# Four-layer image model, selective scan: partitions re-tiled from 128 channels to 4 state groups by 32 channels

## Chip, cores and metric

The kernel runs on one core of a Trainium2 chip. The metric is the device time of one execution in microseconds (us). The kernel before takes 22,114.64 us, the median of three runs (22,108.16 to 22,117.55).

## The reference

The input is `x` of 8 images, 56 x 56 pixels, 192 channels, in fp32. Four layers follow each other, each added to its input after a group normalisation: a gated Toeplitz layer, window attention, a depthwise 3x3 convolution, and a selective scan (384 inner channels `d`, 16 states `n`, 4 scan directions `k`). The change touches the last one:

```python
delta = jax.nn.softplus(delta + delta_bias[None, :, :, None])
dA = jnp.exp(delta[:, :, :, None, :] * A[None, :, :, :, None])
dBu = (delta * u)[:, :, :, None, :] * Bm[:, :, None, :, :]
def comb(e1, e2):
    a1, b1 = e1
    a2, b2 = e2
    return (a1 * a2, a2 * b1 + b2)
_, hs = jax.lax.associative_scan(comb, (dA, dBu), axis=-1)
y = jnp.einsum('bkdnl,bknl->bkdl', hs, Cm)
return y + Dp[None, :, :, None] * u
```

So for each channel and each state there is one recurrence along 3,136 tokens; B and C depend on state and token, not on the channel; delta and u depend on channel and token, not on the state; at the end the 16 states are summed.

## The kernel before

**The first phase** does the Toeplitz layer's transforms for all images and, beside them, the `front` of image 0. **The scan phase** then goes through 224 chunks (8 images, 4 directions called slots, 7 chunks of `CH` = 448 tokens). A chunk has 3 blocks `d` of 128 channels and 8 pairs `k` of states: 5,376 pairs in all, 24 to a chunk. One (chunk, d), that is 8 pairs, is called a block here; there are 672.

**One pair** is one tile of 128 channels by 2 states x 448 tokens:

- `inject` (L1000, GpSimd): `ring` = du x B. `ring` has 6 buffers; it runs two pairs ahead (`ahead`).
- `decay` (L1017, ScalarE): two Exp of delta, with the state's A as scale, into `ps_a` in PSUM (2 buffers), one pair ahead.
- `scan` (L1026, VectorE): the recurrence, in place in `ps_a` or in `ring`.
- `times_c` (L1032): `hc` = states x C, on VectorE, and on GpSimd for k in (1, 4, 6), where it is issued one pair later. `hc` has 4 buffers.
- `add_up` (L1047, TensorE): two matmuls by the identity add both states into `ps_y`, 16 per block. It is issued two pairs later.
- `sums` (L1057, L1059, VectorE): adds `ps_y` to `ysum`, once a block. `keep_state` (L1039) and `initial` (L1007) are small ScalarE copies.

**Its inputs** come through SyncE's DMA queue, in the order of the program. B and C are loaded broadcast: `load_bc` (L973) copies two state rows to all 128 partitions, once for each pair. `load_delta` (L984) brings delta of a chunk, `load_xc` (L978) brings u, and `times_x` (L988, GpSimd, 1 per block) makes du = delta x u.

**Beside the scan** runs the `front` of the next image: `gate`, `attention`, `conv2`, `inner`, and `steps`, which makes B, C (`bc_d`) and delta (`dl_d`) in DRAM, 14 chunk steps per image; Softplus is at L883 and the stores of delta at L886. `finish` normalises and projects the image before. Both are Python generators. A planner (`Parts`) keeps a modelled clock for each engine, and after each pair it inserts as many of their pieces as fit in its limits; nothing is scheduled at run time, each engine executes its instructions in program order. The planner counts `add_up` as 1.1 us of TensorE per pair. Its check of whether a piece fits looks at VectorE, ScalarE and TensorE, not at GpSimd.

Of the kernel before, what the change touches and what calls it, by code (L numbers as in the profile page):

```python
# [15 lines left out]
F32 = mybir.dt.float32  # L16
AF = mybir.ActivationFunctionType
# [6 lines left out]
L = H * W  # L24
# [3 lines left out]
CH = 448  # L28
# [8 lines left out]
NP = NS // NG  # L37
SLAB, SLAB_F = 10048, 2688
# [44 lines left out]
def model(ctx: ExitStack, tc: tile.TileContext, a: dict, out: bass.AP):  # L83
# [5 lines left out]
    def load_const(pool, name, eng=None):  # L89
        t = pool.tile(list(a[name].shape), F32, name=name + "_sb")  # L90
        (eng or nc.sync).dma_start(out=t, in_=a[name])
        return t
# [18 lines left out]
        for n, shape in (("xc", [128, ND, L]), ("bc", [64, L]))  # L111
    )
    dl_d = [[dram.tile([128, ND, L], F32, name=f"dl{s}_{b}") for b in range(B)] for s in range(4)]
# [181 lines left out]
    with (  # L295
# [5 lines left out]
        ln_g, ln_b, w_out, w_dt = (load_const(wp, n) for n in ("ln_g", "ln_b", "w_out", "w_dt"))  # L301
        negA = load_const(wp, "A_logs")
# [542 lines left out]
        def steps(b):  # L845

            w_x, xc, rc, dl = carve(slab, 128, (2, ND, 128), (2, ND, CH), (2, CH), (2, ND, CH))
            nc.sync.dma_start(out=w_x, in_=a["w_x"])
            todo = [(o, j) for o in (1, 0) for j in range(NCH)]

            def load_x(n):
                o, j = todo[n]
                nc.sync.dma_start(out=xc[:, n % 2], in_=xc_d[o][b][:, :, j * CH : (j + 1) * CH])

            load_x(0)
            yield 0, 0, 8.0
            for n, (o, j) in enumerate(todo):
                tok = slice(j * CH, (j + 1) * CH)
                if n + 1 < len(todo):
                    load_x(n + 1)  # L860
                yield 0, 1
                p = bank()
                for d in range(ND):
                    nc.tensor.matmul(p[:, :CH], w_x[:, o, d, :], xc[:, n % 2, d, :], start=d == 0, stop=d == ND - 1)
                yield 1, 0
                nc.scalar.copy(rc[:, n % 2, :], p[:, :CH])
                nc.sync.dma_start(out=bc_d[o][b][:, tok], in_=rc[64:, n % 2, :])
                for d in range(ND):
                    yield 0, 2
                    held = []  # L870
                    for s in range(2):
                        row = slice(32 * s, 32 * s + R)
                        held.append(bank())
                        nc.tensor.matmul(
                            held[s][:, :CH], w_dt[row, o, d * 128 : (d + 1) * 128], rc[row, n % 2, :], start=True, stop=True
                        )
                    yield 2, 0
                    for s in range(2):
                        nc.scalar.activation(
                            dl[:, s, d, :], held[s][:, :CH], AF.Identity, bias=dt_b[:, 2 * o + s, d : d + 1]  # L880
                        )
                yield 0, 0
                nc.scalar.activation(dl, dl, AF.Softplus)  # L883
                usual_functions()
                for s in range(2):
                    nc.sync.dma_start(out=dl_d[2 * o + s][b][:, :, tok], in_=dl[:, s])  # L886
                made.add((b, o, j))
            yield 0, 0
# [76 lines left out]
        bms, cms, deltas, dus, xcs, states, hss, das, hcs, yps, xds = ({} for _ in range(11))  # L965

        def load_bc(i, k):
            b, slot, j = chunks[i]
            for ts, name, r0 in ((bms, "bm", 0), (cms, "cm", NS)):
                ts[i, k] = bcp.tile([128, NG, CH], F32, name=name)  # L970
                r = slot % 2 * 32 + r0 + NG * k
                src = bc_d[slot // 2][b][r : r + NG, j * CH : (j + 1) * CH]
                nc.sync.dma_start(out=ts[i, k], in_=src.unsqueeze(0).to_broadcast([128, NG, CH]))  # L973

        def load_xc(i, d):
            b, slot, j = chunks[i]
            t = sp.tile([128, CH], F32, name="xcd", bufs=3)
            nc.sync.dma_start(out=t, in_=xc_d[slot // 2][b][:, d, j * CH : (j + 1) * CH])  # L978
            return t

        def load_delta(i):
            b, slot, j = chunks[i]
            delta = deltas[i] = delta2[:, i % 2]
            nc.sync.dma_start(out=delta[:, :, 1 : CH + 1], in_=dl_d[slot][b][:, :, j * CH : (j + 1) * CH])  # L984

        def times_x(i, d):
            du = dus[i, d] = sp.tile([128, 1, CH], F32, name="du", bufs=3)
            nc.gpsimd.tensor_mul(du[:, 0, :], deltas[i][:, d, 1 : CH + 1], xcs.pop((i, d)))  # L988

        def tokens(i):  # L990

            return (slice(0, CH), CH, 0) if chunks[i][1] % 2 else (slice(1, CH + 1), 0, CH)

        def on_pool(d, k):
            return k in (1, 4, 6)

        def inject(g):
            i, d, k = pairs[g]
            hs = hss[g] = ring[:, g % 6]
            nc.gpsimd.tensor_mul(hs[:, :, tokens(i)[0]], dus[i, d].to_broadcast([128, NG, CH]), bms[i, k])  # L1000
# [8 lines left out]
        def decay(g):  # L1009
            i, d, k = pairs[g]  # L1010
            slot = chunks[i][1]
            dA = psa.tile([128, 1024], F32, name="ps_a")
            dA = das[g] = dA[:, : NG * (CH + 1)].rearrange("p (n t) -> p n t", n=NG)
            at = slot % 2
            for n in range(NG):
                c = NG * k + n
                nc.scalar.activation(  # L1017
                    dA[:, n, :], deltas[i][:, d, at : at + CH + 1], AF.Exp, scale=negA[:, slot, d, c : c + 1]
                )
# [8 lines left out]
        def times_c(g):  # L1028
            i, d, k = pairs[g]
            h = hss[g] if on_pool(d, k) else das[g]  # L1030
            hc = hcs[g] = sp.tile([128, NG, CH], F32, name="hc", bufs=4)
            (nc.gpsimd if on_pool(d, k) else nc.vector).tensor_mul(hc, h[:, :, tokens(i)[0]], cms[i, k])  # L1032
# [8 lines left out]
        def add_up(g):  # L1041

            i, d, k = pairs[g]
            if k == 0:
                yps[i, d] = psy.tile([128, 512], F32, name="ps_y")
            for n in range(NG):
                nc.tensor.matmul(  # L1047
                    yps[i, d][:, :CH], ident, hcs[g][:, n, :], start=k + n == 0, stop=k + n == NP + NG - 2
                )
# [105 lines left out]
        bcp = own.enter_context(tc.tile_pool(name="bc", bufs=NP))  # L1155
        ysum = wp2.tile([128, ND, L], F32, name="ysum")
        ring = wp2.tile([128, 6, NG, CH + 1], F32, name="ring")
        delta2 = wp2.tile([128, 2, ND, CH + 2], F32, name="delta2")

        for u in range(2):  # L1160
            nc.gpsimd.memset(delta2[:, u, :, 0 : CH + 2 : CH + 1], 1e30)
# [3 lines left out]
        with tc.manual_schedule():  # L1165
            for k in range(NP):
                load_bc(0, k)
            load_delta(0)
            for d in range(ND):
                xcs[0, d] = load_xc(0, d)  # L1170
                times_x(0, d)
# [10 lines left out]
            def take(g):  # L1182
                times_c(g)
                after = scanned[g], summed[g - 4] if g > 3 else 0.0
                taken[g] = run("P", 2.0, *after) if on_pool(*pairs[g][1:]) else run("D", 1.09, *after)
# [11 lines left out]
            for g, (i, d, k) in enumerate(pairs):  # L1197
# [5 lines left out]
                if more and d == 1 and k == 0:  # L1203
                    b1, slot1, j1 = chunks[i + 1]
                    while (b1, slot1 // 2, j1) not in made:
                        parts.step(anything, ahead_of)
                    load_delta(i + 1)
                    for e in range(2):
                        xcs[i + 1, e] = load_xc(i + 1, e)
                if more and (d, k) == (2, 0):  # L1210
                    xcs[i + 1, 2] = load_xc(i + 1, 2)
                if more and (d, k) in ((1, 6), (1, 7), (2, 6)):
                    times_x(i + 1, k - 6 if d == 1 else 2)
                    run("P", 1.08)
# [17 lines left out]
                if g and pd == ND - 1 and pi + 1 < len(chunks):  # L1232
                    load_bc(pi + 1, pk)
# [17 lines left out]
                if g >= 2:  # L1251
                    add_up(g - 2)
                    summed[g - 2] = run("E", 1.1, taken[g - 2])
            if on_pool(d, k):
                times_c(last)
            for g in (last - 1, last):
                add_up(g)
# [6 lines left out]
def constants():  # L1264
# [22 lines left out]
    return {"ident": np.eye(128, dtype=f), "gmat": gmat, "pos": pos, "masks": masks}  # L1287


def layouts(i):  # L1290
# [47 lines left out]
    a["A_logs"] = np.asarray(i[p + "A_logs"]).reshape(4, ND, 128, NS)[order].transpose(2, 0, 1, 3)  # L1338
# [24 lines left out]
```

## Time and profile before

| what | value |
|---|---|
| median of the runs | 22,114.64 us |
| span of the profiled execution | 22,054.7 us |
| scan phase, first to last scan | 3,429.8 to 22,017.6 us: 18,587.8 us |
| one image of the scan phase, images 0 to 6 | 2,347 to 2,393 us |
| the last image (no front beside it) | 2,030 us |
| VectorE busy in the scan phase | 15,930 us |
| TensorE clock granted, mean | 0.891 |

The page cuts the span into 40 slices and gives the busy tenths of each engine. PE is TensorE's matmuls, PEld its weight loads, DVE is VectorE, ACT ScalarE, POOL GpSimd. An fp32 matmul of the program stands in the trace as two instructions, each with a weight load.

```profile
## 2 busy tenths in 40 slices
PE   7878977788887889888988888788988898887667
...
DVE  2122117997799779987899789977998789977998
...
POOL 0000007987889778987888788878898789878999
PEclk9588868999999989999999999898999999998888
```

From slice 7 on the scan runs. DVE and POOL go up and down together with a period of about 4.3 slices, one image: high while the front is in `gate` and `attention`, low in `conv2`, `inner` and `steps`. In the last slices, without a front, POOL is at its highest and PE at its lowest. The chain of work that ended last covers under 1% of the span here, so it says nothing on the whole; the reading goes by stretches and by waits.

### The profile page before, as it was taken

Reading aid. Unit: us, or ns where it says so; the run is one execution under the profiler, and the core shown is the slowest. Engines: PE = TensorE matmul, PEld = TensorE weight load, DVE = VectorE, ACT = ScalarE, POOL = GpSimd, SP = SyncE. Lnnn points to the kernel's source line nnn. Section 1 sums busy time; section 2 is a strip of 40 time slices with the busy share of each in tenths; the row PEclk is TensorE's granted clock in tenths of the full one; section 3 lists DMA queues with packets and bytes.
Section 4 is the critical chain, followed back from the end, with each engine's and each line's share of the span. In section 5 each row is a group of like instructions: output and inputs, shape, how many; then the busy total and the mean of one; then the engine's idle time right before and its main releaser. Section 6 shows DMA issues by size and latency. Waiting matters only on the chain. (4 is left out here: it accounts for less than half of the span.)

```text
span 22054.7 us, 196675 instructions
## 1 busy us (share of the span) xinstructions
PE 18328.2 (83%) x58396; PEld 9752.3 (44%) x58396; DVE 16637.5 (75%) x13276; ACT 12126.1 (55%) x28153; POOL 16068.5 (73%) x8503
## 2 busy tenths in 40 slices
PE   7878977788887889888988888788988898887667
PEld 4845654334443444344443444344444444343333
DVE  2122117997799779987899789977998789977998
ACT  3125114655666465656665576656565666556554
POOL 0000007987889778987888788878898789878999
PEclk9588868999999989999999999898999999998888
DMA  3832575344644465345644464345534564445433
GB/s 88 239 99 49 177 186 165 122 130 162 185 138 125 145 194 152 121 129 180 185 124 128 159 196 137 123 147 189 159 117 131 176 186 125 126 151 184 129 127 110
DMA packets 2419588, 3249.95 MB, mean 147 GB/s; under 512 B 917598, under 2 KB 2361024, under 8 KB 2387554
## 3 DMA queue, kind: packets, MB, share of 16 engines
q1 hardware_dynamic: 2398292, 3121.12, 46.8%
q0 software_dynamic: 15520, 116.14, 1.4%
q8 instruction: 463, 7.59, 0.1%
q14 instruction: 609, 4.99, 0.1%
q10 hardware_dynamic: 4704, 0.12, 0.0%
HBM read 2661.35 MB, written 575.48 MB: 147 GB/s over the span
## 5 line engine op out<-in xcount | busy, mean ns | idle before, releaser
L1000 POOL TENSOR_TENSOR ring<-du,bm 128x896 f32<-128x896 f32 x5376 | 11104.3, 2092 | 17.3 <-DMA bm<-bc 10.1
L1047 PE MATMUL ps_y<-hc,ident_sb 128*128 128x448 f32 x21504 | 9809.0, 591 | 688.5 <-POOL hc L1032 620.9
L1026 DVE TENSOR_TENSOR_SCAN ps_a<-ps_a,ring 128x898 f32<-128x898 f32 x3360 | 6795.9, 2023 | 756.3 <-ACT ps_a L1017 295.2
L1017 ACT ACTIVATE ps_a<-delta,A_logs_sb 128x449 f32<-128x449 f32 x10752 | 6860.2, 638 | 327.8 <-DVE ring L1026 45.5
L1047 PEld LDWEIGHTS ps_y<-hc,ident_sb 128*128 128x128 f32 x21504 | 4281.7, 207 | 4745.4 <-issue 3574.5
L1032 POOL TENSOR_TENSOR hc<-ring,cm 128x896 f32<-128x896 f32 x2016 | 3947.5, 1958 | 2086.0 <-DVE ring L1026 991.9
L1032 DVE TENSOR_TENSOR hc<-ps_a,cm 128x896 f32<-128x896 f32 x3360 | 3668.4, 1092 | 1166.5 <-PE ps_y L1047 880.1
L1026 DVE TENSOR_TENSOR_SCAN ring<-ps_a,ring 128x898 f32<-128x898 f32 x2016 | 4063.3, 2016 | 276.6 <-ACT state L1039 121.0
L1039 ACT COPY state<-ps_a 128x2 f32<-128x2 f32 x3359 | 529.9, 158 | 4120.2 <-DVE hc L1032 4111.2
L278 DVE COPY tzx<-ps_tz 112x448 f32<-112x448 f32 x432 | 269.9, 625 | 1421.9 <-PE ps_tz L272 1289.2
L286 POOL DMA_DIRECT2D o<-tzx x192 | 97.4, 514 | 1686.4 <-DVE tzx L278 1552.5
L272 PE MATMUL ps_tz<-tzx,tm 112*112 112x112 f32 x4608 | 1031.7, 404 | 287.2 <-DMA tm<-ext 272.9
L272 PEld LDWEIGHTS ps_tz<-tzx,tm 112*112 112x112 f32 x4608 | 1028.1, 319 | 326.6 <-issue 320.5
L815 PE MATMUL ps_f<-slab 128*128 128x448 f32 x2646 | 1092.8, 549 | 55.3 <-DMA slab<-dg_d 48.1
L645 PE MATMUL ps_f<-ident_sb,slab 98*98 98x98 f32 x1344 | 335.8, 315 | 558.1 <-ACT slab L638 558.1
L747 PE MATMUL ps_f<-slab 96*96 96x448 f32 x1764 | 729.8, 549 | 42.5 <-DVE slab L734 42.5
L815 PEld LDWEIGHTS ps_f<-slab 128*128 128x128 f32 x2646 | 508.5, 193 | 555.8 <-issue 502.2
L77 PE MATMUL ps_f<-slab 96*96 96x448 f32 (+6 forms) x2306 | 737.8, 501 | 9.3 <-DMA slab<-x 4.1
L988 POOL TENSOR_TENSOR du<-delta,xcd 128x448 f32<-128x448 f32 x672 | 711.0, 1058 | 22.2 <-DMA slab<-in_x_dram 22.2
L1039 ACT COPY state<-ring 128x2 f32<-128x2 f32 x2016 | 378.7, 188 | 609.7 <-DVE ring L1026 581.0
L630 ACT ACTIVATE slab<-slab,mxs 98x98 f32<-98x98 f32 x1344 | 487.6, 364 | 357.8 <-DVE mxs L627 357.8
L482 PE MATMUL ps_f<-ident_sb,slab 112*96 112x112 f32 x4704 | 531.1, 267 | 138.3 <-DVE slab L490 95.0
(218 smaller groups left out, 16966.9 us busy)
## 6 DMA issues: line engine op xcount, KB each, us to landing
bm<-bc SPq DMA_DIRECT2D x1792, 448.0 KB
cm<-bc SPq DMA_DIRECT2D x1792, 448.0 KB
xcd<-xc SPq DMA_DIRECT2D x840, 224.0 KB
dl<-slab SPq DMA_DIRECT2D x224, 672.0 KB
delta<-dl SPq DMA_DIRECT2D x224, 672.0 KB
tzx<-qv SPq DMA_DIRECT2D x192, 588.0 KB
o<-tzx POOLq DMA_DIRECT2D x192, 588.0 KB, 14.2
slab<-x SPq DMA_DIRECT2D x224, 336.0 KB
```

What stands on the lines that cost most here:

```text
L77: return f(*args, **kw)
L272: nc.tensor.matmul(po[:, c, :], t[:, :, c2 + c], x[:, :, c1 + c2 + c], start=True, stop=True)
L482: nc.tensor.matmul(p[:CP, t * TT : (t + 1) * TT], ot[:, n % 2, i, t, c % 2 * CP : c % 2 * CP + CP], ident[:TT, :TT], start=i == 0, stop=i ...
L747: nc.tensor.matmul(p[:CP, :CH], dg[:, k, t, :], xp[:, u, k, dy : dy + 8, dx : dx + W], start=t == 0, stop=t == 8,)
L815: nc.tensor.matmul(p[:, :CH], dg[:, t, :], xp[:, 8 * j + dy : 8 * j + dy + 8, dx : dx + W], start=t == 0, stop=t == 8,)
L988: nc.gpsimd.tensor_mul(du[:, 0, :], deltas[i][:, d, 1 : CH + 1], xcs.pop((i, d)))
L1000: nc.gpsimd.tensor_mul(hs[:, :, tokens(i)[0]], dus[i, d].to_broadcast([128, NG, CH]), bms[i, k])
L1017: nc.scalar.activation(dA[:, n, :], deltas[i][:, d, at : at + CH + 1], AF.Exp, scale=negA[:, slot, d, c : c + 1])
L1026: nc.vector.tensor_tensor_scan(h, dA, hs, 0.0, ALU.mult, ALU.add)
L1032: (nc.gpsimd if on_pool(d, k) else nc.vector).tensor_mul(hc, h[:, :, tokens(i)[0]], cms[i, k])
L1039: nc.scalar.copy(states[i][:, d, NG * k : NG * k + NG], h[:, :, tokens(i)[2]])
L1047: nc.tensor.matmul(yps[i, d][:, :CH], ident, hcs[g][:, n, :], start=k + n == 0, stop=k + n == NP + NG - 2)
```

## The change

A scan tile now holds 4 groups of states by 32 channels on its 128 partitions (partition = 32 x group + channel). `k` runs over 4 quarters of the 128 channels (`k % 4`) and 2 pairs of states within the groups (`k // 4`), so that a block still has 8 pairs of the same size.

- The sum over states: `sel` (128 x 32, four stacked identities) sums the four groups. `add_up` runs once for four pairs and issues 8 matmuls, as many as four calls did before, each into its own 32 partitions of `ps_y` (a column strip of TensorE), quarter by quarter in turn. `hc` gets 8 buffers. The planner counts 1.6 us per call.
- B and C: `load_bc` runs once per chunk, 2 DMAs of 896 KB: each partition gets the four rows of its own group.
- delta: `load_delta` runs four times a block, one block ahead, 448.5 KB each: 32 channels' rows, four times over. A row holds delta, one value 1e30 and du.
- du is made in `steps`, two GpSimd products of 128 x 1,344 per chunk step, and stored in DRAM beside delta; `times_x` and its loads of u are gone. The stores of delta are twice as large.

Core of the diff:

```diff
-            w_x, xc, rc, dl = carve(slab, 128, (2, ND, 128), (2, ND, CH), (2, CH), (2, ND, CH))
+            w_x, xc, rc, dl = carve(slab, 128, (2, ND, 128), (2, ND, CH), (2, CH), (2, ND, DU))
+            delta = dl[:, :, :, :CH]
...
-                nc.scalar.activation(dl, dl, AF.Softplus)
+                nc.scalar.activation(delta, delta, AF.Softplus)
                 usual_functions()
                 for s in range(2):
-                    nc.sync.dma_start(out=dl_d[2 * o + s][b][:, :, tok], in_=dl[:, s])
+                    yield 0, 0
+                    nc.gpsimd.tensor_mul(dl[:, s, :, CH + 1 :], delta[:, s], xc[:, n % 2])
+                    nc.sync.dma_start(out=dl_d[2 * o + s][b][j], in_=dl[:, s])
...
-        def load_bc(i, k):
+        def load_bc(i):
             b, slot, j = chunks[i]
-            for ts, name, r0 in ((bms, "bm", 0), (cms, "cm", NS)):
...
+            for u in range(2):
+                src = bass.AP(
+                    rows.tensor, rows.offset + u * NS * CH, [[NS // NA * CH, NA], [0, DC], [1, NS // NA * CH]]
+                )
+                nc.sync.dma_start(out=t[:, u].rearrange("p q t -> p (q t)"), in_=src)
...
+        def load_delta(i, d, m):
             b, slot, j = chunks[i]
+            rows = dl_d[slot][b][j, m * DC : (m + 1) * DC, d, :]
+            src = bass.AP(rows.tensor, rows.offset, [[0, NA], [ND * DU, DC], [1, DU]])
+            nc.sync.dma_start(out=delta2[:, (ND * i + d) % 2, m, 1:], in_=src)
...
-        def times_x(i, d):
-            du = dus[i, d] = sp.tile([128, 1, CH], F32, name="du", bufs=3)
-            nc.gpsimd.tensor_mul(du[:, 0, :], deltas[i][:, d, 1 : CH + 1], xcs.pop((i, d)))
...
         def add_up(g):
             i, d, k = pairs[g]
-            if k == 0:
+            if k < NJ:
                 yps[i, d] = psy.tile([128, 512], F32, name="ps_y")
             for n in range(NG):
-                nc.tensor.matmul(
-                    yps[i, d][:, :CH], ident, hcs[g][:, n, :], start=k + n == 0, stop=k + n == NP + NG - 2
-                )
+                for m in range(NJ):
+                    nc.tensor.matmul(
+                        yps[i, d][m * DC : (m + 1) * DC, :CH],
+                        sel,
+                        hcs[g - NJ + 1 + m][:, n, :],
+                        start=k < NJ and n == 0,
+                        stop=k >= NJ and n == NG - 1,
+                    )
...
-                if more and d == 1 and k == 0:
+                if more and (d, k) == (ND - 1, 0):
                     b1, slot1, j1 = chunks[i + 1]
                     while (b1, slot1 // 2, j1) not in made:
                         parts.step(anything, ahead_of)
-                    load_delta(i + 1)
...
+                    load_bc(i + 1)
+                if k < NJ and (more or d < ND - 1):
+                    load_delta(*((i, d + 1) if d < ND - 1 else (i + 1, 0)), k)
...
-                if g >= 2:
-                    add_up(g - 2)
-                    summed[g - 2] = run("E", 1.1, taken[g - 2])
+                if g and g % NJ == 0:
+                    add_up(g - 1)
+                    summed[g - NJ : g] = [run("E", 1.6, *taken[g - NJ : g])] * NJ
...
+    sel = np.tile(np.eye(DC, dtype=f), (NA, 1))
```

## Prediction

> **What bounds the kernel now.** I read the busy time by stretches first, then the groups of instructions, then the waits, then the timeline of one wait. The columns after the window are its length, then busy us (instructions) of PE, PEld, DVE, ACT and POOL, the granted clock, the DMA share and GB/s.
>
> ```profile
> 20600.00:21500.00 900.00, 611.53 (x1251) 272.29 (x1252) 849.12 (x548) 453.94 (x1042) 900.00 (x469) 0.86 0.39 127
> 11200.00:11800.00 600.00, 476.83 (x1711) 235.85 (x1710) 566.89 (x474) 412.36 (x1209) 550.65 (x286) 0.93 0.39 122
> 12300.00:12700.00 400.00, 341.83 (x946) 179.06 (x947) 282.65 (x188) 221.11 (x453) 308.77 (x163) 0.93 0.51 166
> 11950.00:12100.00 150.00, 145.70 (x380) 65.53 (x380) 133.80 (x108) 56.78 (x136) 111.85 (x58) 0.99 0.30 93
> ```
>
> Without a front (first row) POOL is busy all the time; 313 feeds in 900 us make 23.0 us per block. Beside attention (second) DVE is busy 94%, 25.2 us per block. Beside conv2 and inner (last two) DVE and POOL both fall back and PE is at 85 to 97%: by the scans' start times blocks take 25 to 35 us there, and 30 beside `steps`. An image with a front takes 2,347 to 2,393 us, 84 blocks at 23.0 would be 1,932.
>
> ```profile
> L1000 POOL TENSOR_TENSOR ring<-du,bm 128x896 f32<-128x896 f32 x5376 | 11104.3, 2092 | 17.3 <-DMA bm<-bc 10.1
> L1047 PE MATMUL ps_y<-hc,ident_sb 128*128 128x448 f32 x21504 | 9809.0, 591 | 688.5 <-POOL hc L1032 620.9
> L1032 POOL TENSOR_TENSOR hc<-ring,cm 128x896 f32<-128x896 f32 x2016 | 3947.5, 1958 | 2086.0 <-DVE ring L1026 991.9
> L1032 DVE TENSOR_TENSOR hc<-ps_a,cm 128x896 f32<-128x896 f32 x3360 | 3668.4, 1092 | 1166.5 <-PE ps_y L1047 880.1
> ```
>
> `add_up` is over half of PE's busy time. DVE's products stand idle 1,166 us, 880 of it until `add_up` gives an `hc` buffer back; POOL's wait 477 us for the same. How such a wait looks:
>
> ```profile
> 12696.38 3.58 PE L1047 MATMUL ps_y<-hc,ident_sb 128*128 128x448 f32 x8
> 12698.54 1.77 POOL L1032 TENSOR_TENSOR hc<-ring,cm 128x896 f32<-128x896 f32 x1 [7.82 <-PE ps_y L1047]
> 12700.00 1.09 DVE L1032 TENSOR_TENSOR hc<-ps_a,cm 128x896 f32<-128x896 f32 x1 [7.13 <-PE ps_y L1047]
> ```
>
> PE's order is full of front matmuls that the planner thinks cheaper than they are (an `add_up` of four instructions streams 4 x 375 ns = 1.5 us and is planned at 1.1), so PE falls behind, and both elementwise engines stop. ACT waits too: on PE for front results some 1,220 us in the scan phase (L824 529, L802 198, L469 141, L866 140, L799 125, L879 87), with `decay` queued behind. In the scan phase of 18,588 us DVE is busy 15,930 and idle 2,657.
>
> **The change, part by part.** *Sums on PE.* Today 21,504 instructions x 375 ns (start to start) = 8.06 ms. Whether four strips run together is shown by three of them: attention's L657 writes strips of 32 columns.
>
> ```profile
> 4027.01 1.09 PE L1047 MATMUL ps_y<-hc,ident_sb 128*128 128x448 f32 x2
> 4028.03 0.54 PE L657 MATMUL ps_f<-slab 98*32 98x98 f32 x12
> 4028.50 1.02 PE L1047 MATMUL ps_y<-hc,ident_sb 128*128 128x448 f32 x2
> ```
>
> The twelve start in four rounds of three, 7 ns apart inside a round and 84 to 108 ns from round to round; one alone would stream about 82 (375 x 98/448). So the strips overlap fully, and the two halves of an fp32 matmul don't spoil it. A call of the new `add_up` is 16 instructions in 4 rounds of 4: 4 x 375 + 12 x 7 = 1.58 us. Going into L657 from L1047 takes 469 ns instead of 375, back 175 instead of 82: +187 ns for both. 1,344 calls x 1.77 us = 2.4 ms: PE loses 5.7 ms of work. Bounds: if strips didn't overlap at all, 16 x 375 + 187 ns = 6.2 us, 8.3 ms and no gain; I take the overlap, the row being the same kind of strip with more rows or columns.
>
> The Trainium skill, page TensorE: Matmul & The Clock Gate, Part 3, measured only 2.38x for three column tiles, where this trace runs three strips in the time of one. By it a call would take about 2.1 us (an estimate), 0.4 ms more in all and hidden as before; the trace decides.
>
> The last stretch, where PE is 68% busy, has a granted clock of 0.86, the denser ones 0.93 to 0.99; the trace's clock records are 1.0 or 0.5, in steps of 3.41 us. The same page, Part 1, has a rule that speaks against this change: a PE idle for some 3.4 us drops to half its clock. By it the emptier PE would run front matmuls up to twice as long; if a tenth of the front's PE time (15,534 - 9,806 = 5,728 us) came onto the path so, the sum would be some 570 us higher (an estimate). The trace shows no such price even in the last stretch, so I leave it out of the sum.
>
> *What this frees.* With 1.77 us in each 11 us and 8 `hc` buffers a block's products have four pairs of slack. I put the `hc` waits of DVE (880) and its own waits for front results on PE (about 200: L756 94, L912 53, L947, L501, L490) at 0; the low end of the gain keeps a tenth.
>
> *B and C.* 7,168 KB a chunk in 16 DMAs become 1,792 KB in 2; delta and u, 1,344 KB in 4, become 5,382 KB in 12. Sum 8.5 to 7.2 MB. Packets of 1,792 bytes took 89 ns on the mean, 12,544 bytes 541: time goes with bytes, so queues are loaded less. A strip of delta is issued six pairs, 17 us, ahead of the feed that reads it, as B and C are today, and POOL waits 10 us for those in all. Cost 0; the price if that cover fails is a rival below.
>
> *du.* POOL loses 708 us in the scan phase (669 x 1.06) and gains 98 x 2 products of 1,344 elements, between 2.33 and 2.40 ns an element by the rows of 896 (2,092) and 672 (1,613): 3.15 us, 617 us. New is a wait: the product stands in POOL's order right behind Softplus, the planner doesn't ask POOL, and behind it wait the feeds, then DVE's scan. ACT needs 1.28 us for the table, 2.45 for Softplus, and may have a `decay` (1.3) ahead of them; so 0 to 5.0 us, I take 3, near the row of `finish` below (338/108): 3 x 98 = 294. The like wait in `finish` (L927, L934 on ACT) costs POOL 564 us today. The store of delta waits for POOL on SP's queue, and the next delta strips behind it, inside their 17 us. POOL then has 15,920 - 708 + 617 + 564 + 294 = 16,687 us: close under DVE.
>
> *First phase.* The 14 steps of image 0 store 19.3 MB more; at the 189 GB/s of that stretch 102 us if nothing hides it, with 14 x 6.3 = 88 of POOL; or 0. They lie beside the Toeplitz transforms, so +60. The first loads before the scan (ACT waits 122 us there for C) shrink by 4.9 MB: -20. So 3,470.
>
> **Sum.** DVE's work 15,930, unchanged. Gaps between its instructions as in the POOL-bound stretch: idle 51 minus 29 until POOL's `ring`, in 849, 2.6%: 413. Its waits on ACT come to 790 today (L1017 360, L1039 248, L1007 182); ACT is late partly because PE is, so half, 395 (ends 0 and 790). DMA and small front waits 270 stay. POOL's lateness, today 160 at the scan, 100 (0 to 600). Scan phase 17,108; with 3,470 before and 37 after, span 20,615. The runs' median lies 60 above the profiled span: **20,675**, 6.5% less. All low ends: 3,410 + 15,930 + 413 + 270 + 37 + 60 = 20,120. All high ends (first phase 102 + 88, a tenth of 1,080 PE waits): 3,620 + 15,930 + 413 + 790 + 270 + 108 + 600 + 37 + 60 = 21,830.
>
> **Rivals.** *POOL becomes the bound at `steps`* (0.17). The planner inserts both products together: 5.0 + 6.3 us ahead of the next feed, against two pairs (5.7) of lead, so DVE loses up to 98 x 5.6 = 550, and with SP's queue held as long, 98 x 11.3 = 1,107: 21,225 to 21,780. For it: POOL 100% busy in the first row. Against it: du's old work goes.
> *Strips don't overlap* (0.04). PE keeps its load plus 1,344 x 0.187 = 251 us; only the buffers help: 21,900 to 22,300. L657 speaks against it.
> *Better: waits vanish* (0.09): 19,850 to 20,120, DVE with its gaps alone, the 270 gone too.
> *Slower: delta lands late* (0.08). 671 blocks each need four strips and, once a chunk, 1,792 KB of B and C in the same 17 us. From 2.15 us of wait per block the gain of 1,440 is gone; at 2.5 the time is 22,350. For it: SP already stands up to 42.8 us behind front stores (16.6 on the mean at L765). Against it: today's burst is 896 KB per pair, more than the new one.
>
> **How the numbers follow.** The forecast, POOL and DVE level with PE out of the way, has 0.62, its own range 20,200 to 21,200. With the better end and most of the POOL rival the range is 19,950 to 21,750. A run of this kernel tells about 0.2% (44 us) from no change: faster 0.62 + 0.17 + 0.09 + half of the strips' 0.04 = 0.90, same 0.01, slower 0.08 + 0.01 = 0.09.
>
> **What would show it.** `add_up` in rounds of four 375 ns apart, PE under 55% busy; DVE's `hc` waits on `ps_y` near 0; blocks beside inner under 26 us; POOL waiting on Softplus a few us, 98 times; images of about 2,170 us, the last one near 1,950. I am wrong if POOL's feeds wait for DMA, if PE is as busy as now, or if POOL's idle time behind ACT exceeds 1.5 ms.

## Result, and the profile after

The changed kernel takes 24,642.68 us, the median of four runs (24,631.64 to 24,652.04). The kernel before, run beside it, takes 22,115.31 us. The ratio is 1.115 (95% interval 1.113 to 1.116): the change costs 2,527 us, where the prediction had a gain of 1,440. It is 3,968 us above the forecast of 20,675.

The busy tenths of the 40 slices, from the page of the changed kernel:

```profile
PE   8699855565656555565556555565656655554534
...
DVE  2122148875798568965797568865797669865997
...
POOL 0000047767687667767686667766686667766887
PEclk8588766676767766676767776676767766776656
DMA  4733653234323343234323443234323443234222
```

PE is down as forecast, but POOL and DVE are lower too in nearly all of the scan phase, and even in the last slices, without a front, POOL no longer reaches 9. These three engines have become emptier, and ACT is busy for 49% of the span, so the bound is none of them. Its groups of instructions (after the bar: busy us, mean ns of one, then the idle time ahead of them and what ended most of it) say what they wait for:

```profile
L1020 POOL TENSOR_TENSOR ring<-delta,bcm 128x896 f32<-128x896 f32 x5376 | 10252.5, 1931 | 1729.3 <-DMA delta<-dl 1576.7
L1045 DVE TENSOR_TENSOR_SCAN ps_a<-ps_a,ring 128x898 f32<-128x898 f32 x3360 | 6798.8, 2023 | 1963.8 <-ACT ps_a L1036 757.4
L1036 ACT ACTIVATE ps_a<-delta,A_logs_sb 128x449 f32<-128x449 f32 x10752 | 6860.2, 638 | 859.4 <-DMA delta<-dl 477.5
...
L1067 PE MATMUL ps_y<-hc,sel_sb 128*32 128x448 f32 x21504 | 4106.7, 774 | 1811.6 <-POOL hc L1051 1362.6
...
L1051 DVE TENSOR_TENSOR hc<-ps_a,bcm 128x896 f32<-128x896 f32 x3360 | 3668.5, 1092 | 176.8 <-DVE ps_a L1045 3.6
...
L1081 DVE SCALAR_TENSOR_TENSOR ysum<-xcd,Dsum,ps_y 128x448 f32<-128x448 f32 x168 | 176.1, 1048 | 1354.6 <-DMA xcd<-xc 1351.0
```

The old wait is gone: DVE's products (L1051), which stood 880 us for an `hc` buffer, no longer wait for PE, and `add_up` is now the one that waits, for its input. New is that what is loaded comes late: the feeds (L1020) and `decay` (L1036) wait for delta, 1,577 and 478 us, and DVE waits 1,351 us for `xcd`, the u that `sums` reads. That load stands on the same queue as delta's; in the kernel before, DVE waited 39 us for it.

The scan phase in one table (us). Busy times come from the windows of that phase, DVE's waits from its waits view, added up by what ended them; "interleaved" is the first experiment.

| | before | changed | interleaved |
|---|---|---|---|
| length | 18,588 | 21,226 | 18,222 |
| DVE busy | 15,930 | 15,947 | 15,950 |
| DVE waits for PE | 1,085 | 387 | 222 |
| DVE waits for ACT | 911 | 2,154 | 1,246 |
| DVE waits for POOL | 171 | 708 | 316 |
| DVE waits for DMA | 167 | 1,780 | 243 |
| POOL busy | 15,920 | 14,977 | 14,968 |
| PE busy, granted clock | 15,534, 0.92 | 12,050, 0.69 | 11,987, 0.73 |

DVE does the same work. The change takes some 700 us of PE's waits away and adds 1,613 of DMA's, and ACT's and POOL's grow while these two wait for delta as well.

**Where the loads run.** In the trace's packet records, a delta load of 448.5 KB is 128 packets of 3,588 bytes, 141 ns each on the median. In the last stretch of the changed kernel (23,200 to 24,200 us) such packets are in flight 82% of the time, 3.7 at once on the mean and exactly 4 for most of it. In the kernel before (20,600 to 21,500 us) its 1,792-byte packets (B and C above all) run 13.7 at once, most often 16. So the new loads run as if over four of the 16 DMA engines; the packet records kept here name no engine, the four is read from the number in flight. In the windows, that is a low DMA share beside engines that wait for DMA (columns as in the prediction; changed kernel):

```profile
23200.00:24200.00 1000.00, 381.98 (x1372) 73.57 (x1372) 910.60 (x589) 489.96 (x1126) 875.39 (x464) 0.59 0.26 104
```

One chunk needs 12 x 128 packets x 141 ns for delta and u and 2 x 128 x 272 ns for B and C: 286 us of packets. Over 16 engines that is 18 us; over four it is 72. In the window above 13.9 chunks pass in 1,000 us, 72 us each, so there the four engines set the pace (POOL's pace before was 69 us, 3 x 23.0). Beside a front a chunk takes 97 us on the mean (an image of 2,687 to 2,747 us, 28 chunks). Over the scan phase 3.2 packets of these loads and 2.4 others are in flight on the mean; if the others spread evenly over 16 engines, the four are busy for 3.2 + 2.4/4 = 3.8 of 4 (an estimate).

What the loads of delta and those of B and C have in common is a first entry of count four in the source pattern: `[[0, NA], [ND * DU, DC], [1, DU]]` has four copies outermost, and B and C's has the four groups. The Trainium skill, page DMA: Bandwidth & Descriptors, states this in Rules for kernel authors: an outermost dimension smaller than 16, such as a leading zero-stride broadcast, "confines the whole DMA to at most c engines"; the trace agrees, with c = 4 and 3.7 packets in flight. The prediction didn't use that rule.

### The profile page after: what moved, and what is told of

Same layout as the page of the kernel before. It is cut to its first block, busy times and chain, and to the rows that moved or that the text cites. A ratio compares the mean times of both kernels' runs of the same rounds, so it can differ in the third digit from the quotient of the medians.

```text
span 24646.0 us, 193825 instructions
## 1 busy us (share of the span) xinstructions
PE 14827.5 (60%) x58396; PEld 7007.7 (28%) x58396; DVE 16653.6 (68%) x13277; ACT 12107.2 (49%) x28161; POOL 15201.5 (62%) x8054
## 5 line engine op out<-in xcount | busy, mean ns | idle before, releaser
L1020 POOL TENSOR_TENSOR ring<-delta,bcm 128x896 f32<-128x896 f32 x5376 | 10252.5, 1931 | 1729.3 <-DMA delta<-dl 1576.7
L1036 ACT ACTIVATE ps_a<-delta,A_logs_sb 128x449 f32<-128x449 f32 x10752 | 6860.2, 638 | 859.4 <-DMA delta<-dl 477.5
L1051 POOL TENSOR_TENSOR hc<-ring,bcm 128x896 f32<-128x896 f32 x2016 | 3937.3, 1953 | 3441.4 <-DVE ring L1045 2789.6
L1067 PE MATMUL ps_y<-hc,sel_sb 128*32 128x448 f32 x21504 | 4106.7, 774 | 1811.6 <-POOL hc L1051 1362.6
L1051 DVE TENSOR_TENSOR hc<-ps_a,bcm 128x896 f32<-128x896 f32 x3360 | 3668.5, 1092 | 176.8 <-DVE ps_a L1045 3.6
L1067 PEld LDWEIGHTS ps_y<-hc,sel_sb 128*32 128x32 f32 x21504 | 866.0, 138 | 4428.4 <-POOL hc L1051 1816.8
L882 PE MATMUL ps_f<-slab,w_dt_sb 12*128 12x448 f32 x1176 | 658.3, 898 | 956.4 <-ACT slab L887 604.0
L822 PE MATMUL ps_f<-slab 128*128 128x448 f32 x2646 | 1086.6, 563 | 229.0 <-DMA slab<-dg_d 200.6
L1081 DVE SCALAR_TENSOR_TENSOR ysum<-xcd,Dsum,ps_y 128x448 f32<-128x448 f32 x168 | 176.1, 1048 | 1354.6 <-DMA xcd<-xc 1351.0
L801 PE MATMUL ps_f<-slab 96*128 96x448 f32 x1176 | 636.1, 691 | 504.4 <-DMA slab<-x 486.1
L489 PEld LDWEIGHTS ps_f<-ident_sb,slab 112*96 112x96 f32 x4704 | 625.7, 208 | 865.1 <-DVE slab L497 592.4
L600 PE MATMUL ps_f<-slab 32*98 32x98 f32 x2688 | 442.9, 343 | 705.3 <-DVE slab L605 499.2
## 6 DMA issues: line engine op xcount, KB each, us to landing
delta<-dl SPq DMA_DIRECT2D x2688, 448.5 KB
```

What stands on the lines that cost most here:

```text
L489: nc.tensor.matmul(p[:CP, t * TT : (t + 1) * TT], ot[:, n % 2, i, t, c % 2 * CP : c % 2 * CP + CP], ident[:TT, :TT], start=i == 0, stop=i ...
L801: nc.tensor.matmul(p[:, :CH], w_in[:, k, u * 128 : (u + 1) * 128], x[:, j % 2, k, :], start=k == 0, stop=k == 1)
L822: nc.tensor.matmul(p[:, :CH], dg[:, t, :], xp[:, 8 * j + dy : 8 * j + dy + 8, dx : dx + W], start=t == 0, stop=t == 8,)
L882: nc.tensor.matmul(held[s][:, :CH], w_dt[row, o, d * 128 : (d + 1) * 128], rc[row, n % 2, :], start=True, stop=True)
L1020: nc.gpsimd.tensor_mul(hs[:, :, tokens(i)[0]], du, bc_of(i, k, 0))
L1036: nc.scalar.activation(dA[:, n, :], delta_of(i, d, k, 0), AF.Exp, scale=negA[:, slot, d, k % NJ, q : q + 1])
```

## Experiments

**Interleaved: the same work with 32 outermost.** Partition = 4 x channel + group instead of 32 x group + channel, so that the loads' patterns start with 32 channels. Sizes, packets and instructions stay.

```diff
-[[NS // NA * CH, NA], [0, DC], [1, NS // NA * CH]]
+[[0, DC], [NS // NA * CH, NA], [1, NS // NA * CH]]
...
-[[0, NA], [ND * DU, DC], [1, DU]]
+[[ND * DU, DC], [0, NA], [1, DU]]
...
-    sel = np.tile(np.eye(DC, dtype=f), (NA, 1))
+    sel = np.repeat(np.eye(DC, dtype=f), NA, axis=0)
```

> The changed kernel with the partition order turned round (partition = 4 x channel + group instead of 32 x group + channel), so that the source of each delta and B/C load has 32 instead of 4 as its outermost count; bytes, packets, number and order of the loads are the same. Theory A (loads with an outermost count of 4 run on 4 of the 16 DMA engines and land late): packets of 3,588 bytes in flight rise from 4 to about 16, POOL's wait for delta falls from 1,577 us to under 150, and the time to about 20,700 us, where the forecast had it. Rival B (six pairs of lead are too short for loads in SP's order, however fast): over 24,000 us. Rival C (the emptier TensorE's lower clock, 0.70 instead of 0.89, slows the front): no change, about 24,600 us. Rival D (POOL waits for Softplus): about 24,000 us or more, as the products stay.

Measured: 21,629.02 us, ratio to the kernel before 0.979 (0.978 to 0.981). Its page:

```profile
L1020 POOL TENSOR_TENSOR ring<-delta,bcm 128x896 f32<-128x896 f32 x5376 | 10241.5, 1931 | 25.8 <-ACT state L1058 21.4
L1045 DVE TENSOR_TENSOR_SCAN ps_a<-ps_a,ring 128x898 f32<-128x898 f32 x3360 | 6796.7, 2023 | 1000.7 <-ACT ps_a L1036 391.5
...
L1067 PE MATMUL ps_y<-hc,sel_sb 128*32 128x448 f32 x21504 | 4201.5, 762 | 1107.8 <-POOL hc L1051 789.6
```

The feed's wait for delta, 1,577 us, is 4, and DVE's for `xcd`, 1,351, is 81. The same 3,588-byte packets are now in flight 34% of the time (20,600 to 21,500 us), 11.9 at once on the mean and most often 16. The order of the first two entries was worth 3,014 us: the whole loss, and a gain of 2.1% under it. Rivals B, C and D, which had 24,000 us or more, are out as causes of the loss. Theory A's time of 20,700 us wasn't reached: 929 us are missing, which the sections below take up. SP's issues became shorter too: one delta load took SP 1.44 us on the median in the changed kernel and 0.52 here. For B and C the median is the same, 0.59 us, and the mean went from 1.93 to 0.64; two issues of the long kind, first in the changed kernel, then two in this one (start, us, count):

```profile
23428.37 8.54 SPq L986 DMA_DIRECT2D bcm<-bc  x2
```

```profile
20933.58 1.20 SPq L986 DMA_DIRECT2D bcm<-bc  x2
```

**The same in the old kernel.** The kernel before, with B and C stored as `[NCH, 64, CH]` (each pair's two rows in one packet) and broadcast by 4 x 32, then by 32 x 4: one difference.

```diff
-                src = bc_d[slot // 2][b][r : r + NG, j * CH : (j + 1) * CH]
+                src = bc_d[slot // 2][b][j, r : r + NG, :]
+                src = bass.AP(src.tensor, src.offset, [[0, 4], [0, 32], [1, NG * CH]])
```

> The kernel before, with B and C stored chunk by chunk so that a pair's two rows lie together, and loaded with a broadcast written as 4 x 32 copies (outermost count 4). Nothing else of the change is in it. Theory A: 7,168 KB a chunk go through 4 engines; at 3,584 bytes in about 141 ns each that is some 100 GB/s or 72 us a chunk before any other load, so the kernel becomes bound by its loads: 24,500 us or more. Rivals B, C, D: within 1% of 22,115 us.

> The same as the run before it, with the broadcast written as 32 x 4 copies (outermost count 32). Theory A: within 1% of the kernel before, 21,900 to 22,300 us; about 16 packets in flight. Rivals B, C, D: the same, and no different from the run with 4 x 32.

Measured: 29,701.43 us (ratio 1.345) with 4 outermost, 22,035.75 us (0.998; 0.997 to 0.999) with 32. Its 3,584-byte packets are 4.1 at once in the first (28,000 to 29,000 us) and 13.8 in the second (20,600 to 21,500). The feed in the two pages, 4 x 32 first:

```profile
L1001 POOL TENSOR_TENSOR ring<-du,bm 128x896 f32<-128x896 f32 x5376 | 11121.5, 2088 | 7451.4 <-DMA bm<-bc 7176.8
```

```profile
L1001 POOL TENSOR_TENSOR ring<-du,bm 128x896 f32<-128x896 f32 x5376 | 11090.3, 2088 | 7.2 <-DMA bm<-bc 5.8
```

So the cause belongs to the pattern, not to the re-tiling, the strips or the layout of rows: both read the same bytes in the same packets.

**Which of the two loads.** The changed kernel with each delta load cut into four DMAs of 32 partitions (32 channels outermost), B and C left; and its mirror, B and C cut, delta left.

```diff
-            src = bass.AP(rows.tensor, rows.offset, [[0, NA], [ND * DU, DC], [1, DU]])
-            nc.sync.dma_start(out=delta2[:, (ND * i + d) % 2, m, 1:], in_=src)
+            for q in range(NA):
+                nc.sync.dma_start(out=delta2[q * DC : (q + 1) * DC, (ND * i + d) % 2, m, 1:], in_=rows)
```

> The changed kernel with each delta load cut into four DMAs of 32 partitions (outermost count 32), B and C left with an outermost count of 4. Theory A: delta was the larger part (5,382 of 7,174 KB a chunk), so most of the loss goes: 20,700 to 21,500 us, with 48 instead of 12 issues a chunk on SP (36 x about 0.4 = 14 us of some 70 us of SP's time). If the loads of B and C hold the queue as much as delta does: 22,500 us or more. Rivals B, C, D: 24,000 us or more.

> The changed kernel with only its B and C loads mended: each cut into four DMAs of 32 partitions (8 a chunk in place of 2), the delta loads left with the leading four copies. It is the mirror of the run that mended delta alone (22,858 us, 1,785 under the changed kernel; both mended by the other partition order: 21,629). Theory A (each delta load has four engines and takes some 4.5 us, so delta is the larger part): GpSimd's feeds go on waiting for delta, over 700 us, and the time is 23,000 to 24,200 us. Theory B (the B and C loads, 896 KB on four engines each, hold the queue and delta is only late behind them): the feed's wait falls under 300 us and the time under 22,600 us.

Measured: 22,857.57 us with delta mended (1,785 less than the changed kernel), 23,217.15 with B and C mended (1,426 less). Each time only the mended load spreads: with delta mended its packets are 10.4 at once and those of B and C 3.8 (21,500 to 22,500 us), in the mirror 3.9 and 8.4 (22,000 to 22,900). Waits for delta and `xcd`, first with delta mended, then with B and C mended:

```profile
DVE ysum L1081 <- DMA xcd<-xc: 636.9, 67, 27.2
POOL ring L1020 <- DMA delta<-dl: 536.3, 102, 15.8
```

```profile
DVE ysum L1082 <- DMA xcd<-xc: 773.6, 121, 21.7
...
POOL ring L1021 <- DMA delta<-dl: 266.5, 109, 8.4
```

The two parts add up to 3,211, about the 3,014 of both. With delta mended, the time was neither the 20,700 to 21,500 us of Theory A nor the 24,000 of the rivals, but the branch in which B and C hold the queue as much. In the mirror the time was Theory A's and the feed's wait Theory B's (266, under 300): with delta alone on four engines the lateness shows at `xcd` and on ACT more than at the feed. And the feed waits 536 us for delta although delta's own loads are mended, which fits B and C holding the queue ahead of it. Neither load is "the" cause; one queue carries both.

**What the strips are worth.** Interleaved, with the 16 matmuls of a call 128 wide (`sel` padded with zeros, all into the whole `ps_y`), so that PE's load is as large as before; then also with the planner told 6.2 us for it instead of 1.6.

```diff
-                        yps[i, d][m * DC : (m + 1) * DC, :CH],
-                        sel,
+                        yps[i, d][:, :CH],
+                        sel[:, m * 128 : (m + 1) * 128],
```

> The kernel with the partition order turned round, but each of the 16 matmuls of a block's sum is 128 columns wide again (the selector padded with zeros), so no strips run together; instructions, their number, order and the planner's costs are the same otherwise. It puts back TensorE's old load: 16 instead of 4 rounds of 375 ns a call, about 5.7 ms in all. Theory (the strips bring the gain over the kernel before): beside inner and steps TensorE is the bound again, 22,200 us or more. If relief of TensorE is worth nothing now, because ScalarE and VectorE set the pace: within 150 us of 21,629.

> The interleaved layout with full-width sums (the 16 matmuls of a call 128 wide, as in the run with full-width sums), and the planner now told their real cost, 6.2 us a call instead of 1.6. That run took 23,704 us, 2,075 more than with strips, but its planner crowded TensorE. Theory A: most of those 2,075 us were the crowding, and the strips themselves are worth what the old wait for hc buffers and PE's lateness cost, 400 to 1,000 us: 22,000 to 22,700 us, the wait of the elementwise engines for hc under 500 us. Theory B: TensorE's streaming time itself is what costs, whatever the plan: over 23,200 us.

Measured: 23,703.76 us and, with the planner told, 24,280.9. The sums in the page of the first, and a POOL wait of the second from its waits view:

```profile
L1067 PE MATMUL ps_y<-hc,sel_sb 128*128 128x448 f32 x21504 | 9521.4, 600 | 632.9 <-POOL hc L1051 383.5
```

```profile
POOL slab L895 <- ACT slab L891: 3247.8, 90, 448.6
```

With the strips PE's share of the sums is 4,202 us instead of 9,521 and the time 2,075 less. With the padded sums the time is that of the theory that the strips bring the gain, and the granted clock is back at 0.86, from 0.73. The second run contradicted its Theory A: told 6.2 us, the planner places the front otherwise, POOL stands at a product of `steps` up to 449 us, and DVE waits 1,545 us for loads of one of the front's weights (`w_in`). That this is because the planner sees PE full and puts the front off is argued, not shown. So 2,075 us is what the strips are worth in this plan; a value free of the plan wasn't found, and the old kernel carried the same load better, in pieces of four instructions.

**The du products.** Interleaved, without the products in `steps`.

> The interleaved layout with the du products in steps left out (the half of each row that holds du is filled with 0.5 once per image; the stores and loads keep their sizes), so the work left out is 196 GpSimd products of 2.87 us, 558 us, and the wait of 201 us in front of them. Theory A (products on GpSimd behind Softplus are what makes the stretch beside steps slower than before, 2,446 against 2,128 us): that stretch falls to 2,200 us or less and the total to 21,250 to 21,400 us. Theory B (the doubled stores of delta and ScalarE's waits behind them do it): the stretch stays above 2,350 us and the total above 21,530 us.

Measured: 21,396.97 us, 232 less than interleaved; the stretch beside `steps` is some 258 us shorter. DVE's wait for the feed, interleaved first:

```profile
DVE ps_a L1045 <- POOL ring L1020: 208.9, 108, 8.2
```

```profile
DVE ps_a L1045 <- POOL ring L1020: 36.0, 38, 2.9
```

This is Theory A. ACT's wait for the stores of delta, 303 us, falls to 87 with stores of the same size, so that wait too belongs to the product ahead of the store.

**Other ways to lose that wait.** Delta stored right after Softplus, du by itself after its product; and a planner that also asks whether POOL is late:

```diff
+                    nc.sync.dma_start(out=dl_d[2 * o + s][b][j][:, :, : CH + 1], in_=dl[:, s, :, : CH + 1])
+                for s in range(2):
                     nc.gpsimd.tensor_mul(dl[:, s, :, CH + 1 :], delta[:, s], xc[:, n % 2])
-                    nc.sync.dma_start(out=dl_d[2 * o + s][b][j], in_=dl[:, s])
+                    nc.sync.dma_start(out=dl_d[2 * o + s][b][j][:, :, CH + 1 :], in_=dl[:, s, :, CH + 1 :])
```

```diff
+                    if engine == "P" and at > t["P"] + limit.get("P", 1e9) + grace:
+                        return False
...
-                parts.step({"A": max(n2, fed[g + 2]) - 0.7, "E": n1 + 5.0, "D": 0.2})
+                parts.step({"A": max(n2, fed[g + 2]) - 0.7, "E": n1 + 5.0, "D": 0.2, "P": 0.5})
```

> The kernel with the partition order turned round, and in steps delta is stored right after Softplus, apart from du, which is stored after its product. Theory: ScalarE's next step waits 303 us for the common store of delta and du (27 us in the kernel before); stored early, this wait falls under 80 us, and the time by 100 to 300 us, to 21,330 to 21,530. If that wait is covered by others, no change beyond 50 us.

> The kernel with the partition order turned round (21,629 us), and one rule more in the planner: a piece with GpSimd work goes in only when its input is ready within 0.5 us of GpSimd's modelled clock. Rival D (GpSimd stands behind Softplus and ScalarE in steps and finish, and scans wait for the feeds): POOL's waits on ACT, 201 us at the products of du and 248 at finish, fall by half or more, and the time by 150 to 500 us, to 21,130 to 21,480. If ScalarE's long pieces are what holds the scan beside steps, POOL's waits fall and the time stays within 100 us of 21,629.

Measured: 21,820.04 us (191 more than interleaved) and 21,688.6 (60 more; the kernel before, run beside these two, took 22,107 us, 21 more than beside interleaved). With the stores apart the wait moves: POOL's product now waits 270 us for the store of delta. With POOL asked, the product's wait for Softplus is 254 us against 201, where it should have halved. Neither is a remedy.

**Why ACT is late.** Two tries at the 1,246 us of DVE waits on ACT that interleaved has: the planner's cost of a matmul raised from 1.25 to 1.7 ns per column, and both Silu of `inner` left out with their table loads.

```diff
-    TIMES = {"tensor": ("E", 0.04, 1.25e-3), "scalar": ("A", 0.2, 0.83e-3),
+    TIMES = {"tensor": ("E", 0.04, 1.7e-3), "scalar": ("A", 0.2, 0.83e-3),
```

> The kernel with the partition order turned round, and the planner counts a matmul at 1.7 instead of 1.25 ns a column, nearer to the measured 375 ns for each of the two instructions of 448 columns at the granted clock of 0.73. Rival C and the planner (ScalarE stops for front results that TensorE delivers later than planned, at a lower clock): ScalarE's waits on L822 and L801 (450 us) halve, and the time falls by 100 to 300 us. If the lost time is in ScalarE's own long pieces: within 100 us of 21,629.

> The interleaved layout with both Silu of inner left out with their table loads (48 pieces in the program). Theory A (the scan's new waits on ScalarE, some 1,100 us, come from long ScalarE pieces of the front): the stretch beside inner falls from 3,492 to under 3,350 us and the scan's waits on ScalarE by 100 us or more; total 21,420 to 21,520 us. Theory B (these waits are passed on from TensorE and DMA through short front pieces): the stretch falls by less than the left-out work's own ScalarE time, under 60 us, total above 21,570 us.

Measured: 21,843.41 us with the higher cost (214 more), DVE's waits on ACT 1,518, and ACT's waits on L822 and L801 480 us against 470, not halved: a higher cost for PE in the plan doesn't help ACT. Without Silu 21,410.7 us, 218 less, and the stretch beside `inner` some 230 to 250 us shorter, by how its ends are taken. The time is about Theory A's (9 us under its range), its mechanism isn't: DVE's waits on ACT fall only from 1,246 to 1,166, and the stretch holds some five blocks fewer, of 125. So the long pieces seem to cost mainly through the length of the front; what makes ACT late stays open.

## Why the prediction was wrong

**The step that failed** is "B and C / delta": "time goes with bytes, so queues are loaded less … Cost 0". Its duration per packet was right (3,588 bytes took 141 ns on the median, between its rows). What it took for granted was that packets run on all 16 engines as in the trace of before. With a count of four outermost they run on four, 72 us of a chunk instead of 18. The kernel with the order exchanged gives 3,014 of the 3,968 us back by which the forecast was missed; the other 954 are taken apart below. The lead of 17 us was no cover, since it is a latency and the shortage was of throughput: one chunk late, every chunk late.

**The slower rival** "delta lands late" (0.08) had the place and the wrong reason: it put the lateness on SP's order and lead, priced it at 2.5 us per block where 3,014 us are 4.5, and didn't see `xcd`, the largest single new wait on DVE. Its sign, POOL's feeds waiting for DMA, is what appeared.

**The sums on PE** were right. In the trace the 16 matmuls of a call start in four rounds of four, 7 ns apart in a round and 376 ns from round to round at full clock. DVE's wait for `hc` went from 880 to 0. But PE's busy time in the scan phase fell by 3.5 ms (interleaved), not 5.7: the emptier PE ran at a granted clock of 0.73 instead of 0.92 (about 0.75 us from round to round where the clock was half), and its other work went from 5,728 to 7,786 us. "PE under 55% busy" was missed for that (60% of the span in the changed kernel, 68% in interleaved). The prediction had named the half-clock rule of the Trainium skill, page TensorE: Matmul & The Clock Gate, Part 1, and left it out of the sum; the drop came. What it costs at the end wasn't isolated.

**With the loads mended**, the forecast is the row to hold against interleaved: scan phase 17,108 forecast, 18,222 measured, 1,114 more. The gaps between DVE's instructions were smaller than forecast (some 245 against 413). The second miss, and the largest term of the 1,114, is "ACT is late partly because PE is, so half, 395": at the scan ACT's waits are 1,077 us, up from 790. Beside `inner`, where DVE's waits for `hc` were 615 us of idle time and are gone, ACT's rose from 342 to 508. POOL's lateness, 100 forecast with ends 0 and 600, was 316, of which the run without products removed 261. Waits for DMA and for the front on DVE, 270 forecast, were 634 (243 on DMA, 169 on ACT outside the scan, and 222 on PE, where the prediction put its 200 us of front results at 0). Against the 1,114 stand 94 us that the first phase was shorter than forecast, and the 60 us that the sum added from the profiled span to the median: here the median lies 5 us below the span.

**The rival that POOL becomes the bound at `steps`** was right in the wait and too dear: the products cost 232 us, not 550. POOL's sum of 16,687 us held 858 of waits and 15,829 of work; 14,968 of work were measured. The difference of 861 is about what the feeds saved, which took 1,931 ns instead of the 2,092 of before (5,376 of them). Nothing in the prediction foresaw that: POOL's margin was luck. **The first phase** was forecast at 3,470 us and ends at 3,384.5: no cost of the larger stores shows there (it ended at 3,429.8 before). **Image lengths**, forecast 2,170 and 1,950 for the last, were 2,687 to 2,747 and 2,247, and 2,297 to 2,326 and 1,986 in interleaved.

## To carry to other kernels

Before a load is priced by its bytes, read the first entry of its access pattern. Here four outermost kept 3.7 packets in flight and 32 outermost 11.9, with the same bytes. In this trace the sign was a low DMA share (0.26) together with engines that wait for DMA, and the count of packets in flight at once pointed to the cause. And when the wait that bounds a stretch is removed, the next engine's wait (here ACT's) was better forecast as it stood (790) than halved (395): it became 1,077.

## What the runs showed of the hardware

- GpSimd's feed of 128 x 896 took 2,092 ns on the mean in the kernel before and 2,088 in the old kernel with either broadcast. With the new tiles the mean is 1,931, and the trace of interleaved shows that it is made of two kinds: 1,774 ns for even `k`, 2,087 for odd `k`. Of the feed's operands two alternate with `k`: the `ring` buffer, as in the kernel before, where even and odd feeds take the same, and the row of du, whose starts now lie 898 fp32 values (3,592 bytes) apart. So the start of du's row is the difference that is left; no run moves it alone. It is worth some 860 us of POOL's time.
- The order of two zero-stride entries of a broadcast, 4 x 32 against 32 x 4, made 29,701 us out of 22,036.
- Strips of fp32 matmuls in four column groups ran together: four with outputs of 32 x 448 started 7 ns apart, in the 376 ns that one full-width matmul takes.
